# Layer 0's output projection by seven products, two buffers of q and k, and neighbours by row maxima

## The chip, the cores and the metric

The kernel runs on one core of a Trainium2 chip. The time is that of one execution on the device, in microseconds (us). A core has TensorE (PE: matmuls, with PEld for its weight loads), VectorE (DVE), ScalarE (ACT), GpSimd (POOL) and SyncE (SP), which here only issues DMAs. Each engine runs its own instructions in order and waits for others on semaphores.

## The reference

64 graphs of 256 nodes with 512 features go through two attention layers, each with a layer norm and a ReLU ahead of it and a residual behind it. Layer 0 has 4 heads of 64 and sees the adjacency; layer 1 has 8 heads of 64 and sees the adjacency and the node itself. Cut to what matters:

```python
h = maximum(layernorm(x), 0)                     # [64, 256, 512]
q, k, v = h @ Wq, h @ Wk, h @ Wv                 # 4 heads of 64
sim = where(adj, q k^T / 8, -max)                # a node without neighbours attends to all alike
x = x + softmax(sim) v @ Wo + bo
h = maximum(layernorm(x), 0)
h = layernorm(h) * gamma + beta
q, k, v = split(h @ w_qkv.T)                     # 8 heads of 64
scores = where(adj | eye, q k^T / 8, -1e9)
x = x + softmax(scores) v @ w_out.T + b_out
```

All is float32. A row of layer 0 whose node has no neighbour gives equal weights over all 256 nodes.

## The kernel before

Two graphs make a step, so there are 32 steps. All matmuls are float32, except those on the adjacency, which is turned in bfloat16. Scores are kept transposed, keys on the partitions; a mask of 0 or -1e30 is added (`mask_scores`, L795), then come the exponentials (L800), the sum of the two halves of keys (`key_halves`, L808), the products with v (`weigh`, L817), the sums over keys by a matmul with ones (L837), the reciprocals (`invert`, L847, with a check of the greatest sum, L848), their spread over the partitions by eight DMAs on SP (L859) and the scaling of the output (`normalise`, L864). A pair of heads is a unit: two in layer 0, four in layer 1.

A projection of 512 inputs over two graphs is a 2 x 2 block product, and where the kernel says "by seven products" it is done by a scheme of seven block products for eight. `PRODUCT` names the two blocks of each, `weight_sum` and `act_sums0`, `act_sums1` form the sums of blocks that it needs (L404 to L412), `evacuate` and `accumulate` add each product up from its PSUM bank. `SHARED` lets products 2, 4 and 3 accumulate on the banks of 1, 7 and 5, once those have been evacuated. There are four such banks (`m0` to `m3`), which sums, transposes and products take in turn, and four more for scores. Before the change this scheme serves q and k of both layers, v of layer 1 and the combination of layer 1 (`combine1`); v of layer 0 and the combination of layer 0 (`combine0`) are plain matmuls.

The mask of layer 0 needs to know which nodes have neighbours: `masks` sums the turned adjacency over the keys with a matmul by ones (L517), makes the mask `n0` from it on VectorE (L524), and a row `ne` of 0 and 1 (L527) by which q of layer 0 is multiplied on GpSimd (L694).

The order of the work on PE, DVE, ACT and POOL is written out by hand. `at(period, place, fn)` notes a call at a place on a line of time; a step has the length `PERIOD` of places; the list is sorted by place, and the instructions are issued in that order on each engine. A place is thus an order, not a time. `visit(period, w, prev, cur)` weighs one unit and scores the next: six visits lie in a period, and between them lie the sets of seven products (`at_set`). In one period three steps are in work: step s in its layer 1, step s+1 in its combination of layer 0 and its second norms, step s+2 in its norm, projections and first scores of layer 0. `act`, `sm`, `io`, `stat` are pools of SBUF, in which `bufs` is the number of buffers of a name. After the steps, a flag read from the check of sums starts `general_path`, a plain second program, only if a sum had grown beyond a limit.

Of the kernel before, what the change touches and what calls it, by code (L numbers as in the profile page):

```python
# [315 lines left out]
def fast_path(  # L316
# [38 lines left out]
    stat = ctx.enter_context(tc.tile_pool(name="stat", bufs=4))  # L355
    ps_sc = ctx.enter_context(tc.tile_pool(name="ps_sc", bufs=4, space=bass.MemoryType.PSUM))
# [20 lines left out]
    onesb = const.tile([P, P], BF, name="onesb")  # L377
    nc.vector.memset(onesb, 1.0)
# [17 lines left out]
    B_OF = ((0, 8, 7), (1, 3, 1))  # L396
    PRODUCT = {1: (0, 0), 2: (1, 1), 3: (6, 2), 4: (3, 6), 5: (2, 3), 6: (4, 4), 7: (5, 5)}
# [8 lines left out]
    def act_sums0(b, eng=nc.gpsimd):  # L406
        eng.tensor_tensor(b[:, 3], b[:, 7], b[:, 0], ALU.subtract)

    def act_sums1(b, eng=nc.gpsimd):
        eng.tensor_tensor(b[:, 4], b[:, 2], b[:, 3], ALU.subtract)  # L410
        eng.tensor_tensor(b[:, 5], b[:, 2], b[:, 7], ALU.subtract)
        eng.tensor_tensor(b[:, 6], b[:, 1], b[:, 4], ALU.subtract)  # L412
# [3 lines left out]
    HC, HP1 = NC // 2, PR1 // 2  # L416
    wqk0 = const.tile([P, NB, HC, 2, H0], FP, name="wqk0")
    wv0 = const.tile([P, NC, I0], FP, name="wv0")
    wo0 = const.tile([P, PR0, D], FP, name="wo0")
# [6 lines left out]
    def first_weights():  # L426
        for i in range(2):
            for k, w in enumerate((wq, wk)):
                nc.sync.dma_start(
                    wqk0[:, 2 * i:2 * i + 2, :, k, :].rearrange("p j c o -> p (j c) o"),  # L430
                    w[:, i * H0:(i + 1) * H0].rearrange("(c p) o -> p c o", p=P),
                )
        nc.sync.dma_start(wv0, wv.rearrange("(c p) o -> p c o", p=P))
        nc.sync.dma_start(wo0, wo.rearrange("(c p) o -> p c o", p=P))
        for v, t in ((bo, bo_b), (b_out, bout_b)):
            nc.sync.dma_start(t, bass.AP(tensor=v.tensor, offset=v.offset, ap=[[0, P], [1, D]]))
        gbr = sm.tile([2 * NC, P], FP, name="gbr", tag="inv", bufs=1)
        nc.scalar.dma_start(gbr[:NC], gamma.rearrange("(c p) -> c p", p=P))
        nc.scalar.dma_start(gbr[NC:], beta.rearrange("(c p) -> c p", p=P))
        return gbr  # L440
# [57 lines left out]

    def adjacency_turn(s):
        adb = S[s]["adb"]  # L500
        pa = mm_tile([P, NIC, G, N], BF)
        for g in range(G):
            for kc in range(NIC):
                for ic in range(NIC):
                    nc.tensor.transpose(  # L505
                        pa[:, kc, g, ic * P:(ic + 1) * P],
                        adb[:, g * NIC + ic, kc * P:(kc + 1) * P], identb,
                    )
        S[s]["adT"] = act.tile([P, NIC, G, N], BF, name="adT", tag="ab")
        nc.scalar.copy(S[s]["adT"], pa)  # L510

    def masks(s):
        st = S[s]
        adT = st["adT"]
        dg = mm_tile([P, G, N])
        for kc in range(NIC):
            nc.tensor.matmul(dg, onesb, adT[:, kc], start=(kc == 0), stop=(kc == NIC - 1))  # L517
        n1 = st["n1"] = act.tile([P, NIC, G, N], BF, name="n1", bufs=3)
        n0 = st["n0"] = act.tile([P, NIC, G, N], BF, name="n0")
        ne = st["ne"] = act.tile([P, T], FP, name="ne")  # L520
        nc.gpsimd.tensor_scalar(n1, adT, -1.0, BIG, op0=ALU.add, op1=ALU.mult)

        for kc in range(NIC):
            nc.vector.scalar_tensor_tensor(  # L524
                n0[:, kc], dg, 0.5, n1[:, kc], op0=ALU.is_gt, op1=ALU.mult
            )
        nc.vector.tensor_scalar(ne, dg.rearrange("p g n -> p (g n)"), 1.0, None, op0=ALU.min)  # L527
        for kc in range(NIC):
            v = n1[:, kc, :, kc * P:(kc + 1) * P]
            nc.gpsimd.tensor_tensor(v, v, offdiag, ALU.mult)  # L530


    def moments(mv, src, t):
        bs = stat.tile([P, 6], FP, name="bs")
        nc.vector.bn_stats(bs, src[:, t, :])  # L535
        nc.vector.bn_aggr(mv[:, t, 0:2], bs)

    def row_scales(s, var):

        st = S[s]  # L540
        st["r"] = stat.tile([P, NT], FP, name="r", bufs=3)
        st["mr"] = stat.tile([P, NT], FP, name="mr", bufs=3)
        nc.gpsimd.tensor_tensor(st["r"], var, mhalf, ALU.pow)
        nc.gpsimd.tensor_scalar(
            st["mr"], st["mean"][:, :, 0], -1.0, 0.0, op0=ALU.mult, op1=ALU.add
        )
        nc.gpsimd.tensor_tensor(st["mr"], st["mr"], st["r"], ALU.mult)  # L547
# [8 lines left out]
    def norm0(s, t):  # L556
        st = S[s]
        if t == 0:
            st["mean"] = stat.tile([P, NT, 2], FP, name="mv0", bufs=2)
        moments(st["mean"], st["h"], t)  # L560
        if t == NT - 1:
            ve = stat.tile([P, NT], FP, name="ve0", bufs=2)
            nc.gpsimd.tensor_scalar(
                ve, st["mean"][:, :, 1], EPS, 1.0, op0=ALU.add, op1=ALU.mult
            )
            row_scales(s, ve)
# [3 lines left out]
    def norm1(s, t):  # L570
        st, x1 = S[s], S[s]["xt"]
        if t == 0:
            st["mv"] = stat.tile([P, NT, 3], FP, name="mv1", bufs=2)
            st["mean"] = stat.tile([P, NT, 2], FP, name="mg", bufs=2)
            st["h"] = act.tile([P, NT, D], FP, name="h")
# [9 lines left out]
    def norm1_rest(s, t):  # L585
        st = S[s]
        mv, mg, h = st["mv"], st["mean"], st["h"]
        moments(mg, h, t)
        if t == NT - 1:
            ve = stat.tile([P, NT], FP, name="ve1", bufs=2)  # L590
# [81 lines left out]
    def project_qk(s, lyr, a, n):  # L672
# [3 lines left out]
        if n == 1:  # L676
            for pr in (a, a + half):
                st["qk", lyr, pr] = sm.tile([P, 2, T], FP, name="qk", bufs=3)
# [53 lines left out]
    def combine0(s, t):  # L732
        st = S[s]
        bank = mm_tile([P, D])
        for pr in range(PR0):
            nc.tensor.matmul(  # L736
                bank, st["oT0"][:, pr, t // NIC, t % NIC * P:(t % NIC + 1) * P], wo0[:, pr, :],
                start=(pr == 0), stop=(pr == PR0 - 1),
            )
        return lambda: nc.vector.tensor_tensor(st["xt"][:, t, :], bank, st["xt"][:, t, :], ALU.add)  # L740

    def combine1(s, n):
        st = S[s]
        if n == 1:
            st["u"] = sm.tile([P, NIC, HD], FP, name="u", bufs=1)
        bank, first = bank_of(st, "c", n, HD)
        wa, ba = PRODUCT[n]
        for t in range(NIC):
            for c in range(HP1):
                nc.tensor.matmul(  # L750
                    bank[:, t, :], st["oT1"][:, ba, c, t * P:(t + 1) * P], wo1[:, wa, c, :],
                    start=first and (t, c) == (0, 0), stop=(t, c) == (NIC - 1, HP1 - 1),
                    skip_group_check=True,
                )
        return lambda: accumulate(n, bank, token_rows(st["xt"], HD), st["u"], s == NSTEP - 1)
# [54 lines left out]
    def weigh(s, lyr, pr, first):  # L810
# [11 lines left out]
        if lyr == 0:  # L822
            if first:
                st["oT0"] = act.tile([P, PR0, G, N], FP, name="oT0")
            dst = st["oT0"][:, pr]
        else:
            if first:
                st["oT1"] = act.tile([P, NB + 1, HP1, N], FP, name="oT1")
            b0, b1, step = B_OF[pr // HP1]
            dst = st["oT1"][:, b0:b1:step, pr % HP1, :]  # L830
# [39 lines left out]
    PERIOD = 6.13  # L870
# [17 lines left out]
    SETC = (1, 5, 2, 6, 7, 3, 4)  # L888

    def visit(period, w, prev, cur):  # L890
# [7 lines left out]
        if 0 <= cur[0] < NSTEP:  # L898
# [4 lines left out]
            at(period, w + 0.18, exponentials, *cur, 1)  # L903
            at(period, w + 0.2, key_halves, *cur, 0)
            at(period, w + 0.3, key_halves, *cur, 1)

    AT_C0, AT_Q0, AT_V0, AT_H1, AT_C1 = 3.0, 3.57, 4.57, 5.13, 5.131
    for s in range(-1, NSTEP):
# [6 lines left out]
        visit(p, AT_Q0 + 2 / 7, (s, 1, 1, False), (s, 1, 3))  # L915
# [8 lines left out]
    for s in range(NSTEP):  # L924
# [6 lines left out]
        for t in range(NT):  # L931
            at(p, 0.5 + 0.4 * t if s != 1 else 1.8 + 0.2 * t, norm0, s, t)
            at(p, 2.3 + 0.1 * t if s != 1 else 2.6 + 0.1 * t, scale_row, s, t)
        at(p, (3.146, 3.584)[s] if s < 2 else 2.2, adjacency_turn, s)
        at(p, (3.3, 3.727)[s] if s < 2 else 2.75, masks, s)
        for c in range(NC):
            at(p, AT_C0 + 0.14 * (c // 2) + 0.001 * c, transpose_h, s, 0, c)
        at(p, AT_C0 + 0.1, lambda s=s: act_sums0(S[s]["hT"]))
        at(p, AT_C0 + 0.2, lambda s=s: act_sums1(S[s]["hT"]))
# [7 lines left out]
        at(p, 1.8 if s else 0.8, first_bias, s)  # L947
        for t in range(NT):
            at_dense(p, AT_C0 + 0.01 + 0.14 * t, 0.14, combine0, s, t)
            at(p, AT_C0 + 0.3 + 0.14 * t, norm1, s, t)  # L950
            at(p, (3.55, 3.7, 4.05, 4.2)[t], norm1_rest, s, t)
            at(p, 3.62 + 0.08 * t, second_bias, s, t)
            at(p, 4.5 + 0.1 * t, scale_row, s, t)
# [10 lines left out]
        if s < NSTEP - 1:  # L964
            at(p, AT_C1 + 0.1, lambda s=s: act_sums1(S[s]["oT1"]))
            at_set(p, AT_C1, SETC, combine1, s)
            at(p, 6.3, store, s)
        else:
            at(p, AT_C1 + 0.4, lambda s=s: act_sums1(S[s]["oT1"], nc.vector))
            at_set(p, AT_C1, (1, 5, 2, 3, 6, 7, 4), combine1, s)  # L970
# [5 lines left out]
    for i in range(4):  # L976
        at(-2, 2.75, weight_sum, nc.vector, wqk0, i)
    at(-2, 3.5, lambda: blocks.extend(weight_loads()))
# [63 lines left out]
```

## Time and profile before

| | before |
|---|---|
| median of 3 runs | 3436.38 us (3435.82 to 3436.41) |
| profiled execution, its time | 3435.47 us |
| its span, first to last instruction | 3433.7 us |
| granted TensorE clock | 0.997 |
| PE busy | 3391.8 us, 99% of the span |
| VectorE, GpSimd, ACT busy | 1916.3, 1919.4, 1245.3 us |
| records of the combinations: L736, L750 | 512 of 128x512, 1792 of 128x256 |
| records of the neighbours' matmul: L517 | 64 of 128x512 |

A record of PE is half a float32 matmul: L736 has 8 matmuls a step and 16 records. Rows of engines overlap: a "busy" of PE runs on into the next row, so what a piece of work takes is read from the start of one row to the start of the next. "L736 PE MATMUL mm<-wo,oT" reads: line 736, engine, operation, what is written and what is read. In the waits, "A <- B" is time in which A's engine stood still until B was done. In the table of stretches, the pairs after the length are busy time and number of instructions of PE, PEld, DVE, ACT and POOL, followed by the clock, the share of the DMA engines and GB/s.

### The profile page before, as it was taken

The page shows a single profiled execution, that of the slowest core. Times are in us where ns is not written, and L with a number is a line of the kernel's source. Part 1 is how long each engine was busy: PE and PEld are TensorE (multiplying, and loading weights), DVE is VectorE, ACT ScalarE, POOL GpSimd, SP SyncE. Part 2 cuts the span into 40 slices and gives each one's busy share as a digit, 9 for nine tenths or more (in the row PEclk, how much of TensorE's full clock was granted, in tenths as well). Part 3 has the DMA queues.
Part 4 walks back from the last instruction along what each step waited for, and adds up shares of the span by engine and source line. Part 5 has one row for each costly group of instructions (what it writes and reads, how often), then busy time and mean ns, then how long its engine had stood idle before and what let it go on. Part 6 is the DMA issues. An engine that isn't in the chain of part 4 may idle for free.

```text
span 3433.7 us, 59040 instructions
## 1 busy us (share of the span) xinstructions
PE 3391.8 (99%) x22658; PEld 2632.4 (77%) x22658; DVE 1916.3 (56%) x3410; ACT 1245.3 (36%) x2197; POOL 1919.4 (56%) x1790
## 2 busy tenths in 40 slices
PE   8999999999999999999999999999999999999998
PEld 6787777787777877777777778777777777787766
DVE  5655556555565555565555655555655556555544
ACT  3433443333333334433333333344333333333321
POOL 4656565565655566555656555565556565555640
PEclk9999999999999999999999999999999999999999
DMA  3111111111011111111111111111111101111011
GB/s 128 40 53 55 43 40 42 55 55 53 27 45 52 54 55 42 41 42 55 53 54 28 45 52 55 55 37 46 42 54 54 53 29 44 53 54 53 17 41 38
DMA packets 147536, 165.96 MB, mean 48 GB/s; under 512 B 43304, under 2 KB 96048, under 8 KB 147248
## 3 DMA queue, kind: packets, MB, share of 16 engines
q1 hardware_dynamic: 144928, 157.79, 15.4%
q8 instruction: 181, 2.97, 0.4%
q10 hardware_dynamic: 2320, 4.33, 0.4%
q14 instruction: 107, 0.88, 0.1%
HBM read 78.12 MB, written 33.55 MB: 33 GB/s over the span
## 4 chain that ended last, share of the span: by engine, by line
PE 97%; DVE 1%; POOL 1%; ACT 0%; issue 0%; DMA 0%; ACTq 0%; SPq 0%; DVEq 0%; POOLq 0%
PE mm L684 34%; PE mm L725 11%; PE mm L750 11%; PE sc L782 10%; PE sc L817 10%; PE mm L711 6%; PE mm L736 6%; PE mm L603 3%; PE mm L837 2%; PE mm L505 0%; PE mm L517 0%; DVE inv L847 0%; DVE bs L535 0%; SPq L859 0%; ACTq L456 0%
## 5 line engine op out<-in xcount | busy, mean ns | idle before, releaser
L808 POOL TENSOR_TENSOR pd<-p 128x512 f32<-128x512 f32 x380 | 477.7, 1272 | 807.1 <-ACT p L800 706.6
L684 PE MATMUL mm<-hT,wqkv 128*128 128x256 f32 x3584 | 802.0, 381 | 0.0
L684 PEld LDWEIGHTS mm<-hT,wqkv 128*128 128x128 f32 x3584 | 673.9, 190 | 111.0 <-issue 20.9
L800 ACT ACTIVATE p<-p 128x512 f32<-128x512 f32 x768 | 458.9, 629 | 458.8 <-DVE p L795 457.9
L847 DVE RECIPROCAL inv<-mm 128x128 f32<-128x128 f32 x384 | 339.7, 926 | 341.8 <-PE mm L837 324.5
L795 DVE TENSOR_TENSOR p<-sc,n 128x512 f32<-128x512 f32 x768 | 481.2, 682 | 4.5 <-PE sc L782 4.5
L831 ACT COPY oT<-sc 128x512 f32<-128x512 f32 x192 | 112.3, 585 | 1021.1 <-PE sc L817 1021.1
L684 PE MATMUL mm<-hT,wqk 128*128 128x256 f32 x1792 | 401.6, 381 | 3.4 <-ACT qk L618 1.5
L750 PE MATMUL mm<-wo,oT 128*128 128x256 f32 x1792 | 398.0, 383 | 5.0 <-DVE oT L864 3.4
L725 PE MATMUL mm<-wqkv,hT 128*128 128x256 f32 x1792 | 395.3, 381 | 0.0
L684 PEld LDWEIGHTS mm<-hT,wqk 128*128 128x128 f32 x1792 | 337.6, 190 | 72.3 <-DVE inv L847 9.9
L782 PE MATMUL sc<-qk 64*128 64x256 f32 x3072 | 384.9, 390 | 1.9 <-ACT oT L831 1.4
L750 PEld LDWEIGHTS mm<-wo,oT 128*128 128x128 f32 x1792 | 341.4, 192 | 52.6 <-DVE oT L864 4.2
L725 PEld LDWEIGHTS mm<-wqkv,hT 128*128 128x128 f32 x1792 | 338.0, 190 | 55.1 <-issue 10.6
L817 PE MATMUL sc<-p,v 128*32 128x256 f32 x6144 | 374.5, 382 | 5.2 <-ACT p L800 5.2
L782 PEld LDWEIGHTS sc<-qk 64*128 64x128 f32 x3072 | 281.7, 187 | 106.9 <-issue 77.6
L817 PEld LDWEIGHTS sc<-p,v 128*32 128x32 f32 x6144 | 180.4, 109 | 171.0 <-issue 62.2
L864 POOL TENSOR_TENSOR oT<-oT,invb 128x512 f32<-128x512 f32 x190 | 241.8, 1273 | 90.9 <-DMA invb<-inv 86.7
L652 POOL TENSOR_TENSOR xt<-xt,u 128x512 f32<-128x512 f32 x93 | 118.0, 1269 | 245.6 <-DVE xt L645 184.2
L554 ACT ACTIVATE h<-h,mr,r 128x512 f32<-128x512 f32 x252 | 197.4, 808 | 123.9 <-POOL mr L547 123.9
L736 PE MATMUL mm<-wo,oT 128*128 128x512 f32 x512 | 230.4, 593 | 0.0
L711 PE MATMUL mm<-wv,hT 128*128 128x256 f32 x1024 | 230.3, 382 | 0.0
(103 smaller groups left out, 3617.4 us busy)
## 6 DMA issues: line engine op xcount, KB each, us to landing
invb<-inv SPq DMA_DIRECT2D x1532, 32.0 KB, 1.8
xt<-in_x_dram SPq DMA_DIRECT2D x32, 1024.0 KB, 5.4
h<-in_x_dram SPq DMA_DIRECT2D x31, 1024.0 KB, 5.3
out_dram<-xt SPq DMA_DIRECT2D x31, 1024.0 KB, 4.8
ad<-in_adj_dram SPq DMA_DIRECT2D x32, 128.0 KB, 4.4
wr<-in_L_gnn_w_qkv_dram ACTq DMA_DIRECT2D x3, 1024.0 KB, 13.5
h<-in_x_dram SPq DMA_DIRECT2D x4, 256.0 KB, 3.5
wr<-in_L_gnn_w_out_dram ACTq DMA_DIRECT2D x1, 1024.0 KB, 17.3
```

Of the source, the lines that this page charges most:

```text
L684: nc.tensor.matmul(bank[:, k, :], w[:, wa, c, k, a * P:(a + 1) * P], st["hT"][:, ba, c, :], start=first and (k, c) == (0, 0), stop=(k, c) ...
L711: nc.tensor.matmul(bank, st["hT"][:, b0 + t // NIC * step, c % HC, i:i + P], wv0[:, c, :], start=(c == 0), stop=(c == NC - 1),)
L725: nc.tensor.matmul(bank[:, t, :], st["hT"][:, ba, c, t * P:(t + 1) * P], wqkv1[:, wa, c, 2, :], start=first and (t, c) == (0, 0), stop=(t, ...
L736: nc.tensor.matmul(bank, st["oT0"][:, pr, t // NIC, t % NIC * P:(t % NIC + 1) * P], wo0[:, pr, :], start=(pr == 0), stop=(pr == PR0 - 1),)
L750: nc.tensor.matmul(bank[:, t, :], st["oT1"][:, ba, c, t * P:(t + 1) * P], wo1[:, wa, c, :], start=first and (t, c) == (0, 0), stop=(t, c) ...
L782: nc.tensor.matmul(sc[g][e][:, kc, :], qk[rows, 1, k0:k0 + P], qk[rows, 0, g * N:(g + 1) * N], start=True, stop=True,)
L795: nc.vector.tensor_tensor(p[e][:, g], sc[e], neg[:, :, g, :], ALU.add)
L800: nc.scalar.activation(p[e][:, g], p[e][:, g], AF.Exp, scale=SCALE)
L808: engine_of(s, lyr, pr).tensor_tensor(pd[:, e], p[e][:, :, 0, :], p[e][:, :, 1, :], ALU.add)
L817: nc.tensor.matmul(po[r0:r0 + 32, g, :], st[f"v{lyr}"][:, g * NIC + kc, pr * P + r0:pr * P + r0 + 32], p[r0 // DH][:, g, kc, :], start=(kc ...
L847: nc.vector.reciprocal(inv[:, i * P:(i + 1) * P], sums[:, i * P:(i + 1) * P])
L864: engine_of(s, lyr, pr).tensor_tensor(dst, dst, invb, ALU.mult)
```

## The change

The combination of layer 0 is done by seven products too: `combine0` and `combine1` become one `combine`. `wo0` grows to seven blocks of 128x256, of which VectorE makes three at the start, and so does `oT0`, whose sums GpSimd makes before the combination. `oT1` falls from eight blocks to seven. A product of layer 0 is two matmuls of 128x256, and it adds to `xt` through `u`, as in layer 1.

Neighbours are found by a maximum over each row of the adjacency on VectorE (`neighbours`), written to DRAM and read back as one row on all partitions by two DMAs on SP (`spread_neighbours`). The mask `n0` becomes a product on GpSimd.

q and k have two buffers in place of three. The visit that scores the last unit of layer 1 stood two products into the set of q and k of layer 0; it now stands ahead of that set. The places around it move: the four transposes stand together, the combination comes after them, the norms of x1 come behind the visit in the order of rows 2, 3, 0, 1, the second bias goes to the next visit. At the start, `wv0`, `wo0` and the two biases are loaded over ACT's queue.

```diff
-    onesb = const.tile([P, P], BF, name="onesb")
-    nc.vector.memset(onesb, 1.0)
+    O_OF = ((0, 6, 5), (1, 3, 1))
...
-        eng.tensor_tensor(b[:, 3], b[:, 7], b[:, 0], ALU.subtract)
+        eng.tensor_tensor(b[:, 3], b[:, 7 if b.shape[1] > NB else 5], b[:, 0], ALU.subtract)
...
-    wo0 = const.tile([P, PR0, D], FP, name="wo0")
+    wo0 = const.tile([P, NB, HP0, HD], FP, name="wo0")
...
-        nc.sync.dma_start(wv0, wv.rearrange("(c p) o -> p c o", p=P))
-        nc.sync.dma_start(wo0, wo.rearrange("(c p) o -> p c o", p=P))
+        nc.scalar.dma_start(wv0, wv.rearrange("(c p) o -> p c o", p=P))
+        for i in range(2):
+            nc.scalar.dma_start(
+                wo0[:, 2 * i:2 * i + 2].rearrange("p j c o -> p (j c) o"),
+                wo[:, i * HD:(i + 1) * HD].rearrange("(c p) o -> p c o", p=P),
+            )
         for v, t in ((bo, bo_b), (b_out, bout_b)):
-            nc.sync.dma_start(t, ...)
+            nc.scalar.dma_start(t, ...)
...
+    def neighbours(s, g):
+        st = S[s]
+        if g == 0:
+            st["any"] = stat.tile([P, NT], BF, name="any_of", bufs=2)
+        rows = slice(g * NIC, (g + 1) * NIC)
+        nc.vector.tensor_reduce(
+            st["any"][:, rows], st["ad"][:, rows], axis=mybir.AxisListType.X, op=ALU.max
+        )
+
+    def spread_neighbours(s):
+        row = dram.tile([NT, P], BF, name="row")
+        nc.sync.dma_start(row.rearrange("t p -> p t"), S[s]["any"])
+        ne = S[s]["ne"] = act.tile([P, T], BF, name="ne")
+        nc.sync.dma_start(ne, bass.AP(tensor=row.tensor, offset=row.offset, ap=[[0, P], [1, T]]))
...
     def masks(s):
-        dg = mm_tile([P, G, N])
-        for kc in range(NIC):
-            nc.tensor.matmul(dg, onesb, adT[:, kc], start=(kc == 0), stop=(kc == NIC - 1))
...
         for kc in range(NIC):
-            nc.vector.scalar_tensor_tensor(
-                n0[:, kc], dg, 0.5, n1[:, kc], op0=ALU.is_gt, op1=ALU.mult
+            nc.gpsimd.tensor_tensor(
+                n0[:, kc].rearrange("p g n -> p (g n)"),
+                n1[:, kc].rearrange("p g n -> p (g n)"), st["ne"], ALU.mult,
             )
-        nc.vector.tensor_scalar(ne, dg.rearrange("p g n -> p (g n)"), 1.0, None, op0=ALU.min)
...
+    NORM1 = (2, 3, 0, 1)
...
-                st["qk", lyr, pr] = sm.tile([P, 2, T], FP, name="qk", bufs=3)
+                st["qk", lyr, pr] = sm.tile([P, 2, T], FP, name="qk", bufs=2)
...
-    def combine0(s, t):
-        bank = mm_tile([P, D])
-        for pr in range(PR0):
-            nc.tensor.matmul(
-                bank, st["oT0"][:, pr, t // NIC, t % NIC * P:(t % NIC + 1) * P], wo0[:, pr, :],
-                start=(pr == 0), stop=(pr == PR0 - 1),
-            )
-        return lambda: nc.vector.tensor_tensor(st["xt"][:, t, :], bank, st["xt"][:, t, :], ALU.add)
-
-    def combine1(s, n):
+    def combine(s, lyr, n):
+        oT, w, half = st[f"oT{lyr}"], (wo0, wo1)[lyr], (HP0, HP1)[lyr]
         bank, first = bank_of(st, "c", n, HD)
         wa, ba = PRODUCT[n]
         for t in range(NIC):
-            for c in range(HP1):
+            for c in range(half):
                 nc.tensor.matmul(
-                    bank[:, t, :], st["oT1"][:, ba, c, t * P:(t + 1) * P], wo1[:, wa, c, :],
+                    bank[:, t, :], oT[:, ba, c, t * P:(t + 1) * P], w[:, wa, c, :],
...
-    PERIOD = 6.13
+    PERIOD = 6.2
+    SETC0 = (1, 6, 5, 2, 7, 3, 4)
...
-            at(period, w + 0.18, exponentials, *cur, 1)
-            at(period, w + 0.2, key_halves, *cur, 0)
+            at(period, w + 0.22, exponentials, *cur, 1)
+            at(period, w + 0.23, key_halves, *cur, 0)
...
-    AT_C0, AT_Q0, AT_V0, AT_H1, AT_C1 = 3.0, 3.57, 4.57, 5.13, 5.131
+    AT_C0, AT_Q0, AT_V0, AT_H1, AT_C1 = 3.0, 3.64, 4.64, 5.2, 5.201
...
-        visit(p, AT_Q0 + 2 / 7, (s, 1, 1, False), (s, 1, 3))
+        visit(p, AT_Q0, (s, 1, 1, False), (s, 1, 3))
...
+        for g in range(G):
+            at(p, (1.8, 2.7)[s] if s < 2 else 0.58 + 0.14 * g, neighbours, s, g)
+        at(p, (1.81, 2.71)[s] if s < 2 else 0.75, spread_neighbours, s)
...
-            at(p, AT_C0 + 0.14 * (c // 2) + 0.001 * c, transpose_h, s, 0, c)
+            at(p, AT_C0 + 0.001 * c, transpose_h, s, 0, c)
         at(p, AT_C0 + 0.1, lambda s=s: act_sums0(S[s]["hT"]))
-        at(p, AT_C0 + 0.2, lambda s=s: act_sums1(S[s]["hT"]))
+        at(p, AT_C0 + (0.2 if s < 2 else 0.35), lambda s=s: act_sums1(S[s]["hT"]))
...
-            at_dense(p, AT_C0 + 0.01 + 0.14 * t, 0.14, combine0, s, t)
-            at(p, AT_C0 + 0.3 + 0.14 * t, norm1, s, t)
-            at(p, (3.55, 3.7, 4.05, 4.2)[t], norm1_rest, s, t)
-            at(p, 3.62 + 0.08 * t, second_bias, s, t)
-            at(p, 4.5 + 0.1 * t, scale_row, s, t)
+        place = 1.75 if s else 2.48
+        at(p, place, lambda s=s: act_sums0(S[s]["oT0"]))
+        at(p, place + 0.01, lambda s=s: act_sums1(S[s]["oT0"]))
+        for i, n in enumerate(SETC0):
+            at_dense(p, AT_C0 + 0.14 + i / 14, 1 / 14, combine, s, 0, n)
+        for t in range(NT):
+            at(p, (3.79, 3.8, 3.93, 3.94)[t], norm1, s, t)
+            at(p, (4.075, 4.22, 4.23, 4.36)[t], norm1_rest, s, t)
+            at(p, AT_V0 + 0.01 * t, second_bias, s, t)
+            at(p, 4.6 + 0.1 * t, scale_row, s, t)
...
+        at(-2, AT_V0, weight_sum, nc.vector, wo0, i)
```

## The prediction

> **What bounds the kernel now.** I read the page first, then the waits of TensorE, then the busy times of whole steps, then one step in order of time.
>
> ```profile
> PE 3391.8 (99%) x22658; PEld 2632.4 (77%) x22658; DVE 1916.3 (56%) x3410; ACT 1245.3 (36%) x2197; POOL 1919.4 (56%) x1790
> PE 97%; DVE 1%; POOL 1%; ACT 0%; issue 0%; DMA 0%; ACTq 0%; SPq 0%; DVEq 0%; POOLq 0%
> 400.00:505.70 105.70, 105.70 (x713) 82.38 (x712) 59.03 (x105) 39.30 (x69) 61.16 (x58) 1.00 0.16 47
> 1700.00:1805.70 105.70, 105.70 (x710) 82.31 (x709) 59.58 (x107) 38.72 (x68) 60.80 (x58) 1.00 0.16 47
> PE mm L603 <- ACT h L554: 15.9, 7, 10.2
> ```
>
> The chain that ended last is 97% TensorE. In the stretches of one step (columns: length, busy time of PE, PEld, DVE, ACT, POOL, clock, DMA share, GB/s) PE is busy all the time, VectorE and GpSimd 56 to 58%. The waits of PE put 15.9 us on L603, 10.2 of them one wait at the start; between 200 and 3250 us no PE row waits for anything. One step, from L817 at 1199.51 to the same row at 1725.10 five steps on, is 525.59 / 5 = **105.12 us**; 32 of them are 3364, and start and end make up the rest of 3433.7. So work taken from PE is worth its full price, unless another engine then becomes late. The place to look is the timeline of PE around the combination (start, length, counts):
>
> ```profile
> 1725.10 1.93 PE L817 MATMUL sc<-p,v 128*32 128x256 f32 x32
> 1726.86 0.61 PE L837 MATMUL mm<-pd,ones 128*32 128x256 f32 x8
> 1727.40 2.00 PE L782 MATMUL sc<-qk 64*128 64x256 f32 x16
> 1729.33 1.09 PE L603 MATMUL mm<-ident,h 128*128 128x128 f32 x8
> 1730.26 1.88 PE L736 MATMUL mm<-wo,oT 128*128 128x512 f32 x4
> 1731.98 1.04 PE L603 MATMUL mm<-ident,h 128*128 128x128 f32 x8
> 1732.85 5.32 PE L736 MATMUL mm<-wo,oT 128*128 128x512 f32 x12
> 1738.00 3.62 PE L684 MATMUL mm<-hT,wqk 128*128 128x256 f32 x16
> 1741.55 1.93 PE L817 MATMUL sc<-p,v 128*32 128x256 f32 x32
> ...
> 1767.59 12.25 PE L750 MATMUL mm<-wo,oT 128*128 128x256 f32 x56
> 1779.77 1.93 PE L817 MATMUL sc<-p,v 128*32 128x256 f32 x32
> ```
>
> Start to start is what a piece costs: L736 takes 1.72 + 5.15 = 6.87 us, the four transposes 0.93 + 0.87 = 1.80, the layer-1 combination by seven products 12.18.
>
> [...] L808 is 1272 ns in the mean whatever runs beside it. [...] the trace has 1.8 us for `invb`. [...] no 2-byte run is in this trace.
>
> **The change part by part.** Times of a step; "place" is the kernel's own order, one unit some 17 us.
>
> (1) Combination by seven products. PE: 7 products x 2 matmuls of 128x256; in layer 1 four take 12.18/7 = 1.74, so two take 0.87 and the set 6.09: **-0.78**. VectorE: 4 additions of 0.68 go, 6 of 0.69 come, +1.4. ACT: +0.58 (copy into `u`). GpSimd: 3 additions of `u` at 1.27, and 4 block sums of 128x256 before them (no such f32 row; 0.67 by L530, bounds 0.6 and 1.27): +6.5.
>
> (2) Neighbours. PE: L517 goes, 1723.28 - 1722.85 = **-0.43**. VectorE: two L524 (0.69) and L527 (0.68) go; two reductions of 2x256 bytes come, 0.72 each by the slope of the two reductions in the trace (353 at 192, 279 at 128; bounds 0.35 and 1.4). They sit where VectorE idled 1.94 and 1.10 us before evacuations, so nobody waits. GpSimd: two products of 128x512 bf16, 1.27 each (bounds 0.67 and 1.34), in front of the `offdiag` rows, which ended 5.6 us before GpSimd's next work. SP: two DMAs at 0.75, the second waiting for the first. Behind them on SP are the eight `invb` DMAs of visit 1.0 (590 ns each to issue), whose `inv` is ready some 6 us after the first can go. A landing of 1.7 us (fastest `invb`) to 5.4 us (a 1 MB load) fits: cost 0, cover 6 us.
>
> (3) Four transposes in one run instead of two and two: 1.75 (layer 1 at 1765.84 to 1767.59) for 1.80: **-0.05**. But their four evacuations on ACT now precede the first exponentials.
>
> (4) The visit. With two buffers of q and k the scores of unit (1,3) must precede product 1 of the next set; the visit goes ahead of products 1 and 6. Nothing is added: the weighing, the sums, the scores, `invert`, four mask additions, four exponentials and eight DMAs move up 3.5 us on PE, VectorE, ACT and SP, and on GpSimd two key halves and a `normalise`. PE then writes new q and k only after these scores, so the lost buffer costs nothing.
>
> (5) The norms of x1 move behind that visit, rows 2,3,0,1; the second bias (4 x 1.24) moves to the next visit on GpSimd. There it pushes key halves from 8.1 to 12.2 us after the weighing, and block sums of oT1 to 17.2; the product that needs the last of them starts at 22. Free.
>
> (6) Exponentials of graph 1 from +0.18 to +0.22. In visit 2 the `adT` copy (1.01) now precedes them, and the key halves end some 2 us later; GpSimd has that slack until the next `normalise` chain.
>
> Sum of the saving: 0.78 + 0.43 + 0.05 = **1.26 us a step, 40.3 in 32 steps**.
>
> **What comes back.** The stretch of 16.6 us behind the combination is the tight one already (same columns):
>
> ```profile
> 1725.10:1738.00 12.90, 12.90 (x89) 7.47 (x89) 9.78 (x19) 5.75 (x11) 5.51 (x6) 1.00 0.09 22
> 1738.00:1754.60 16.60, 16.60 (x113) 13.03 (x111) 12.45 (x25) 6.76 (x13) 12.94 (x16) 1.00 0.07 18
> ```
>
> I laid the new queues out with the durations of the rows, 0 at the weighing of visit 3.0.
> ACT: `oT` copy 2.0; four relus 4.9 to 7.0; exponentials to 8.05; `u` copy 8.03 to 8.60; exponentials to 9.7. Product 2 reuses the bank of product 1 at 5.98 + 3 x 0.87 = 8.59: PE waits 0.07. Product 7's evacuation must end before product 4, one product (0.87) on: 0.15 (lag in L750's rows) + 0.69 + 0.06 = 0.90, so 0.03 more.
> GpSimd: key halves 9.2 to 11.65, three sums of hT to 15.3, `normalise` to 16.6, `u` additions to 17.85, 19.1, 20.35.
> PE: combination ends at 12.2; weighing, scores, and then the set of q, k for 12.3.
> VectorE from 14.7: `invert` 2.15, four masks 2.40, so the first norm at 19.28, its rows complete at 19.1: a margin of 0.2. Then two norms 1.62, one evacuation 0.60, two norms, one evacuation, three second moments 2.43, evacuation of product 7 at 26.3 to 27.0; PE wants that bank at 27.07. **Margin about zero.**
> The last second moments end at 27.75; then the chain of tiny GpSimd rows and `ne`:
>
> ```profile
> 1752.48 0.19 POOL L591 TENSOR_SCALAR ve<-mv 128x4 f32<-128x4 f32 x1
> ...
> 1753.03 1.02 POOL L543 TENSOR_TENSOR r<-ve,mhalf 128x4 f32<-128x4 f32 x1
> ...
> 1754.55 1.28 POOL L694 TENSOR_TENSOR qk<-qk,ne 128x512 f32<-128x512 f32 x1
> ```
>
> It takes 2.07 + 1.28 and ends at 31.1; the scores that read it start at 31.1, where before they had 1.07 us (1755.83 to 1756.90). Again no margin.
> So 0.1 a step is sure and each tie may cost up to 0.3; I take 0.2 for them together. (0.1 + 0.2) x 30 = 9 back.
>
> **Start.** `wv0`, `wo0` and the biases (1.5 MB) move from SP behind `wqk0` to ACT's queue at once, beside `h`. [...] The trace has 1 MB of `h` landed some 5 us after 0.74; up to 1 MB beside it could delay it by 3. I take +2.5, bounds -1 and 6. SP is held there by the row of neighbours; `h` of step 1 is wanted at 14.1 only.
>
> Sum against the profiled execution: 3435.5 - 40.3 + 9 + 2.5 = 3406.7. It stands 0.9 under the median, so **3408**.
>
> **Rivals.** (A, 0.58) The above: 3396 (nothing back) to 3415. (B, 0.20) The ties give way by 0.6 to 1.0 a step, because VectorE, continuously busy from 14.7 to 30, is the bound of that stretch: 3436.4 - 40.3 + 2.5 + 30 x 0.7 to 1.0 = 3420 to 3429. Against it: PE's waits of a stretch also give VectorE time. (C, 0.14, slower) GpSimd's additions of `u` come behind key halves, three sums and `normalise`, VectorE stops at the first norm for them, behind it stand the evacuations of products 6 and 5, and PE runs out of banks. It decides from 1.2 us a step; if each of the nine GpSimd rows ahead came 0.27 later, or the exponentials 2.4 us later, less the 0.2 of margin, PE would lose about 2.2: 3436.4 + 2.5 + 30 x 2.2 - 40.3 = 3465. For it: margins of 0.2 and 0; against it: rows of 1257 to 1293 ns, no more, in the whole trace. (D, 0.08) B and a bad start cancel the gain: 3430 to 3443. That the new neighbours are not found, so that the second program follows, I give under 0.01.
>
> **Numbers.** About 0.2% (7 us) is what a measurement of this kernel can tell from no change. Faster is A and B, 0.78; same 0.08; slower 0.14. The range, 3397 to 3436, takes A, B and the nearer half of D; A alone is 3396 to 3415.
>
> **What would show it.** Right: L736 and L517 gone; L750 or its successor with 2688 records; a step of 104.0 to 104.4 us; PE with small waits for ACT `u`, the evacuation of product 7, or GpSimd's `qk`, 0.1 to 0.4 us a step. B or C: VectorE rows of the first norm idle before GpSimd's `xt`, PE's L684 waiting for VectorE. Wrong altogether: a step over 105.1 us, or PE waiting for the mask through the row DMA, which I cost at nothing.

## The result, and the profile after

| | before | after |
|---|---|---|
| median | 3436.1 us (3433.78 to 3436.41, 4 runs) | 3526.88 us (3522.1 to 3537.2, 4 runs) |
| profiled execution, its span | 3435.47, 3433.7 us | 3524.76, 3523.0 us |
| PE busy, granted clock | 3391.8 us, 0.997 | 3395.4 us, 0.987 |

The change is **slower**: 1.027 of the time before, 95% interval 1.0246 to 1.0294, or 91 us. The forecast was 3408, a gain of 28 us.

The page of the changed kernel, busy times and the chain that ended last by engine and by line:

```profile
PE 3395.4 (96%) x22978; PEld 2714.9 (77%) x22978; DVE 1933.3 (55%) x3445; ACT 1232.2 (35%) x2229; POOL 2183.6 (62%) x2078
...
PE 72%; DMA 16%; SPq 4%; DVE 3%; issue 2%; POOL 2%; ACT 1%; DVEq 0%; ACTq 0%; POOLq 0%
PE mm L704 26%; PE mm L761 16%; DMA row<-any_of 12%; PE sc L829 7%; PE sc L794 7%; PE mm L731 6%; SPq L870 4%; PE mm L745 3%; PE mm L623 3%; PE mm L848 2%; DVE inv L858 2%; DMA invb<-inv 1%; DMA out_dram<-xt 1%; DMA h<-in_x_dram 0%; POOL pd L820 0%
```

TensorE was 97% of the chain and is 72%. A transfer of 1 KB, the row of neighbours on its way to DRAM, is 12% of it. Before the change TensorE had no wait between 200 and 3250 us, and GpSimd waited little for `invb` there (us in total, times, longest):

```profile
POOL oT L864 <- DMA invb<-inv: 57.6, 67, 2.8
```

The waits of the changed kernel in that window, from TensorE's view of them back to the transfer:

```profile
PE mm L704 <- DVE extremes L859: 60.2, 24, 5.2
...
DVE inv L858 <- DMA invb<-inv: 161.4, 22, 10.4
...
POOL oT L875 <- DMA invb<-inv: 407.3, 36, 17.5
...
SPq L518 <- DMA row<-any_of: 500.5, 28, 21.3
```

Read upwards: SP stands 17.9 us in the mean (500.5 / 28) at its second DMA, `ne<-row`, until the first has landed. The `invb` DMAs are queued behind it. GpSimd's `normalise` waits for them, and so do VectorE's reciprocals, because `inv` has one buffer. On VectorE stand behind the reciprocals the check L859, which reads the bank of sums, the masks and the evacuations; TensorE wants that bank for product 5 of q and k of layer 1. One such place, in the timelines of SP, GpSimd, VectorE and TensorE of the changed kernel (start, length, in brackets the idle time before and its releaser):

```profile
1861.15 0.37 SPq L516 DMA_DIRECT2D row<-any_of  x1
1861.61 0.46 SPq L485 DMA_DIRECT2D ad<-in_adj_dram  x1
1882.28 0.34 SPq L518 DMA_DIRECT2D ne<-row  x1
...
1889.69 1.26 POOL L875 TENSOR_TENSOR oT<-oT,invb 128x512 f32<-128x512 f32 x1 [16.34 <-DMA invb<-inv]
...
1889.70 1.77 DVE L858 RECIPROCAL inv<-mm 128x128 f32<-128x128 f32 x2 [9.21 <-DMA invb<-inv]
...
1887.47 0.61 PE L526 MATMUL mm<-identb,adb 128*128 128x128 bf16 x8
1892.14 10.56 PE L704 MATMUL mm<-hT,wqkv 128*128 128x256 f32 x40 [4.06 <-DVE extremes L859]
```

The `row` DMA is issued at 1861.15, and SP goes on at 1882.28. The cost is more than the wait. The same piece of work, from the scores to the next weighing, without and with it, and the part of the disturbed one that follows the wait, in two pieces (stretches: length, busy time of PE, PEld, DVE, ACT, POOL, clock, DMA share, GB/s):

```profile
1777.57:1792.63 15.06, 14.98 (x85) 12.37 (x81) 7.34 (x12) 7.30 (x12) 11.40 (x14) 1.00 0.12 29
1881.98:1902.63 20.65, 16.59 (x85) 13.63 (x81) 7.34 (x12) 7.31 (x12) 12.54 (x15) 0.92 0.14 33
...
1892.14:1897.00 4.86, 4.86 (x15) 3.95 (x16) 3.55 (x6) 4.43 (x8) 4.63 (x9) 0.65 0.19 47
1897.00:1902.60 5.60, 5.60 (x27) 4.68 (x25) 1.38 (x2) 2.53 (x4) 5.60 (x5) 1.00 0.02 6
```

It takes 5.6 us longer: 4.2 until product 5 starts, and 1.4 because the clock is low behind the wait. The mean of 0.65 over 4.86 us hides two values: from 1892.50 to 1895.80 the granted clock is 0.50, and the record of that stretch is 3.41 us long. All nine waits of 3.3 to 5.2 us in the window came with such a stretch. Of the shorter ones, waits of 1.95 and 2.55 us, which ended at 270.01 and 1466.09, had a clock of 0.50 behind them too (271.20 to 274.40, 1466.10 to 1469.10), and so had one of 2.32, while those of 2.01, 2.23, 2.49 and 2.96 us had not. So in this trace the length of a wait alone does not tell whether the clock falls.

Between 200 and 3250 us the changed kernel has twelve such stretches, 51 us in all; half of that, up to 26 us, is my estimate of what the clock costs. The kernel with a quick row (e2, below) has none. TensorE is busy 2985.1 of these 3050 us, and all 3050.0 in that other kernel, so 65 us are idle. Together that is some 90 of the 98 us by which the changed kernel is slower than that one once the start is over. (Here and below the start ends with the first sums over keys, some 100 us in, that follow the last transposes of weights.)

Where no stall fell, the combination came out close to the forecast. The transposes start at 1796.85, the combination at 1798.65, the next weighing at 1805.00:

```profile
1796.85 1.97 PE L623 MATMUL mm<-ident,h 128*128 128x128 f32 x16
1798.65 6.42 PE L761 MATMUL mm<-wo,oT 128*128 128x256 f32 x28
1805.00 1.93 PE L829 MATMUL sc<-p,v 128*32 128x256 f32 x32
```

The set takes 6.35 us where the plain one took 6.87; 6.09 and 0.1 for its banks were forecast.

The undisturbed piece, 1777.57 to 1792.63, shows how much TensorE could bear. Ahead of it SP issued `row` at 1756.99 and went on at 1773.45, VectorE's reciprocals waited 4.83 us for `invb`, and TensorE waited for nothing. In four such steps SP stood 15.1 to 15.4 us without any wait of TensorE for the check; the 20.2 us behind 1861.15 cost the 4.06.

### The profile page after: what moved, and what is told of

Its sections match the earlier page's. It is cut to its first block, busy times and chain, and to the rows that moved or that the text cites. A ratio compares the mean times of both kernels' runs of the same rounds, so it can differ in the third digit from the quotient of the medians.

```text
span 3523.0 us, 60226 instructions
## 1 busy us (share of the span) xinstructions
PE 3395.4 (96%) x22978; PEld 2714.9 (77%) x22978; DVE 1933.3 (55%) x3445; ACT 1232.2 (35%) x2229; POOL 2183.6 (62%) x2078
## 4 chain that ended last, share of the span: by engine, by line
PE 72%; DMA 16%; SPq 4%; DVE 3%; issue 2%; POOL 2%; ACT 1%; DVEq 0%; ACTq 0%; POOLq 0%
PE mm L704 26%; PE mm L761 16%; DMA row<-any_of 12%; PE sc L829 7%; PE sc L794 7%; PE mm L731 6%; SPq L870 4%; PE mm L745 3%; PE mm L623 3%; PE mm L848 2%; DVE inv L858 2%; DMA invb<-inv 1%; DMA out_dram<-xt 1%; DMA h<-in_x_dram 0%; POOL pd L820 0%
## 5 line engine op out<-in xcount | busy, mean ns | idle before, releaser
L704 PE MATMUL mm<-hT,wqkv 128*128 128x256 f32 x3584 | 823.7, 390 | 62.9 <-DVE extremes L859 60.2
L704 PEld LDWEIGHTS mm<-hT,wqkv 128*128 128x128 f32 x3584 | 688.9, 195 | 185.5 <-issue 82.5
L761 PE MATMUL mm<-wo,oT 128*128 128x256 f32 x2688 | 601.4, 382 | 4.9 <-DVE oT L875 3.2
L761 PEld LDWEIGHTS mm<-wo,oT 128*128 128x128 f32 x2688 | 502.7, 191 | 85.1 <-DVE xt L661 11.1
L672 POOL TENSOR_TENSOR xt<-xt,u 128x512 f32<-128x512 f32 x189 | 239.0, 1272 | 229.9 <-DVE xt L665 184.5
L661 DVE TENSOR_TENSOR xt<-mm,xt 128x512 f32<-128x512 f32 x128 | 88.2, 689 | 338.9 <-PE mm L761 338.8
```

The costliest lines, as they stand in the source:

```text
L672: (nc.vector if last else nc.gpsimd).tensor_tensor(r, r, u, ALU.add)
L704: nc.tensor.matmul(bank[:, k, :], w[:, wa, c, k, a * P:(a + 1) * P], st["hT"][:, ba, c, :], start=first and (k, c) == (0, 0), stop=(k, c) ...
L761: nc.tensor.matmul(bank[:, t, :], oT[:, ba, c, t * P:(t + 1) * P], w[:, wa, c, :], start=first and (t, c) == (0, 0), stop=(t, c) == (NIC - ...
```

## The experiments

My theory after the result: the two-byte row lands late, and this alone is the loss; the rest of the change saves what was forecast. Rivals: the weights on ACT's queue, the new order of the visit, the reductions, or any row sent through DRAM at that place.

### The row alone in the kernel before (e4)

```diff
+        if s >= 2:
+            for g in range(G):
+                at(p, 0.58 + 0.14 * g, neighbours, s, g)
+            at(p, 0.75, spread_neighbours, s)
```

> The kernel before with the row maxima and the two DMAs on SP added from the third step on, their result not used (and only half of the row read back, for room). Theory 1: SP is held for some 16 us a step here too, PE waits 3 to 5 us in most steps, and the time is 3500 to 3580. Theory 2: nobody waits for it, 3436 to 3445.

Measured: 3525.09 us against 3433.64, ratio 1.0258 (1.0241 to 1.0275), so **+91.5 us** for reductions and two DMAs whose result nobody reads. SP and TensorE of this kernel, waits between 200 and 3250 us:

```profile
SPq L515 <- DMA row<-any_of: 490.1, 28, 19.6
...
PE mm L702 <- DVE extremes L866: 48.1, 26, 3.3
```

The same chain, in the old order, without the weights on ACT's queue and without the seven products in layer 0. Reductions and row together are enough; e2 and e9 below keep the reductions and do not have the loss.

### What in the row costs: four forms of it (e5)

The kernel before again, with the row written in a form that changes from step to step, each waited for on SP by a DMA of one element.

```diff
+        if kind == 0:      # near = [4, 128]: 512 pieces of 2 bytes, side by side
+            nc.sync.dma_start(near.rearrange("t p -> p t"), st["any"])
+        elif kind == 1:    # far = [4, 128, 256]: 512 pieces of 2 bytes, 512 bytes apart
+            nc.sync.dma_start(far[:, :, 0].rearrange("t p -> p t"), st["any"])
+        elif kind == 2:    # whole = [128, 4]: 128 pieces of 8 bytes
+            nc.sync.dma_start(whole, st["any"])
+        else:              # half = [2, 128]: 256 pieces of 2 bytes, side by side
+            nc.sync.dma_start(half.rearrange("t p -> p t"), st["any"][:, :2])
```

> The kernel before with the row maxima and a row written by SP from the third step on, its result not used; step by step the row goes out in one of four forms: 512 pieces of 2 bytes side by side in DRAM; 512 pieces of 2 bytes, 512 bytes apart; 128 pieces of 8 bytes; 256 pieces of 2 bytes. SP then reads one element of it back, which shows how long the landing takes. If the landing goes with the number of pieces: 16, 16, some 4 to 5 and 8 to 9 us. If it is that neighbours of 2 bytes fall into the same stretch of DRAM and queue up behind each other: 16, under 5, some 4 and 8 to 9. If it is a fixed price of any write so small: 16 in all four.

SP's waits in this kernel (us in total, times, longest):

```profile
SPq L530 <- DMA half<-any_of: 152.6, 8, 21.6
...
SPq L518 <- DMA near<-any_of: 133.1, 7, 20.0
...
SPq L526 <- DMA whole<-any_of: 38.6, 8, 6.6
...
SPq L522 <- DMA far<-any_of: 29.3, 7, 5.1
```

One run of it took 3509.23 us. The means are 19.1, 19.0, 4.8 and 4.2 us. It is **not the number of pieces**: 512 of them 512 bytes apart land in 4.2, and 256 side by side take as long as 512. I had expected 8 to 9 for the half row, so that part was wrong. What the two slow forms share is runs of 128 two-byte values next to each other.

Nor is it the moving. The trace has a record of every packet. In all four forms the first packet of the row starts 3.6 to 3.8 us after the issue, behind the 1 MB of `xt` that SP issued some 0.5 us earlier, and the last has ended 4.6 to 4.7 us after it. From there until SP is let on pass, in the mean, 15.3 us for the 512 side by side, 15.5 for the 256, 1.7 for the pieces of 8 bytes and 0.6 for those 512 bytes apart. The changed kernel's DMA engines from 1755 to 1776 us show the same, one digit for 0.525 us, tenths busy:

```profile
DMA  7000913799999402002000200100100000000000
```

The row is issued at 1756.99. The nines are `xt` and `ad`. The last packet of 2 bytes ends at 1762.74, after that the engines do nearly nothing, and SP is let on 10.7 us later. Over the 28 rows between 200 and 3250 us it is the same: the last packet ended 4.9 us after the issue in the mean, and 14.0 us more passed (10.7 to 17.6) before SP went on. The time passes after the last packet, and no record shows what fills it.

### The row turned on TensorE (e2)

```diff
+        turned = mm_tile([NT, P], BF)
+        nc.tensor.transpose(turned, S[s]["any"], identb)
+        ne = S[s]["ne"] = act.tile([P, T], BF, name="ne")
+        nc.scalar.copy(ne[:NT, :P], turned)
         row = dram.tile([NT, P], BF, name="row")
-        nc.sync.dma_start(row.rearrange("t p -> p t"), S[s]["any"])
-        ne = S[s]["ne"] = act.tile([P, T], BF, name="ne")
+        nc.sync.dma_start(row, ne[:NT, :P])
```

> The changed kernel with the four columns of row maxima turned on PE (one transpose of 128x4 in bfloat16, a copy on ACT) and written to DRAM as 4 rows of 256 bytes, both DMAs still on SP. Theory 1: the row lands in 2 to 3 us, SP is held no longer than that, and the time is 3398 to 3415, with a start earlier than that of the changed kernel by 10 us or more. If the count of pieces isn't what makes the landing long, it stays near 16 us and the time near 3525. Theory 2: 3490 or more.

Beyond the lines shown, the row goes out at place 0.9 for 0.75, behind `ad`.

Measured: 3413.48 us (3412.77 to 3414.17), ratio **0.994** (0.9923 to 0.9957). Four pieces of 256 bytes land so soon that SP waits 2.4 us in the mean; part of the difference to the forms above is that `xt` goes out some 3 us ahead of the row here, not 0.5. Its waits between 200 and 3250 us, and the chain by engine:

```profile
SPq L521 <- DMA row<-ne: 69.3, 29, 3.2
...
PE 97%; DVE 1%; POOL 1%; DMA 0%; ACT 0%; issue 0%; ACTq 0%; SPq 0%; DVEq 0%; POOLq 0%
```

TensorE waits for nothing in that window, and a step is 1804.86 - 1700.78 = 104.08 us for 105.12. Everything else of the change is still there, so none of the other rivals makes the loss.

### The row in pieces of 8 bytes (e9)

The smallest edit: nothing is added, the row only lies otherwise in DRAM, and GpSimd reads every fourth value.

```diff
-        row = dram.tile([NT, P], BF, name="row")
-        nc.sync.dma_start(row.rearrange("t p -> p t"), S[s]["any"])
+        row = dram.tile([P, NT], BF, name="row")
+        nc.sync.dma_start(row, S[s]["any"])
...
+        S[s]["ne"] = ne.rearrange("p (q t) -> p t q", t=NT)
```

> The changed kernel with one thing altered: the row of neighbours lies in DRAM with the four values of a partition side by side, so it is written in 128 pieces of 8 bytes (4.8 us in the mean with the forms compared side by side), and GpSimd reads its columns in that order, every fourth value. No work is added to TensorE. Theory (the landing of the 2-byte neighbours is the whole loss; my step fails only in the landing that it assumed): 4.8 us lies inside the cover of 6 us that the prediction gave, so TensorE shows no waits behind the spread reciprocals between 200 and 3250 us, and the time is 3408 to 3420. Rival (any row written out and read back in this place holds SP too long): waits behind the spread reciprocals stay, 3450 or more. A second way to miss: GpSimd reads every fourth bf16 value slower than 1.16 us for 128x512; if it takes 1.3 to 2.3 us, q comes later to the scores by that much more, and 1 us a step is lost: some 3440.

Measured: **3412.13 us** (3412.06 to 3414.43) against 3434.83, ratio 0.9938 (0.9921 to 0.9954). SP waits 5.5 us in the mean in the same window, and no engine passes it on to TensorE:

```profile
SPq L518 <- DMA row<-any_of: 160.8, 29, 7.4
```

The landing is longer than that of the turned row and the step is the same, 1804.79 - 1700.71 = 104.08 us. So a wait of 5.5 us in the mean, 7.4 at most, is covered. The 6 us that I had read off were the cover of the `invb` DMAs alone: GpSimd and VectorE have slack behind them, and in the changed kernel TensorE began to wait only where SP stood for more than some 15.5 us. GpSimd's q product takes 1.30 us for 1.16, which nobody waits for.

### Both DMAs on ACT's queue (e1)

```diff
-        nc.sync.dma_start(row.rearrange("t p -> p t"), S[s]["any"])
+        nc.scalar.dma_start(row.rearrange("t p -> p t"), S[s]["any"])
...
-        nc.sync.dma_start(ne, ...)      # right behind it
+        nc.scalar.dma_start(ne, ...)    # at place 1.95 in place of 0.75
```

> The changed kernel with both DMAs of the neighbours on ACT's queue, the one that reads the row back issued at place 1.95 in place of 0.75 (3.25 and 3.7 for the first two steps); the row is still written in 512 pieces of 2 bytes. Theory 1 (SP stands behind the landing of the row, some 16 us a step, so that the eight DMAs of invb, then VectorE at the reciprocals, then PE come late): SP has no wait for the row any more, the waits of PE for VectorE L859 go, and the time falls to 3410 to 3428 (a start some 18 us late is left). Theory 2 (the stretch behind the combination, GpSimd and VectorE, is the cause): 3490 or more. Theory 3 (512 tiny writes hold up the other DMAs on the shared engines): invb lands late all the same, 3480 or more.

The first of the two goes out at 0.9 for 0.75.

Missed: 3451.68 us (3448.18 to 3457.2), ratio 1.0047 (1.003 to 1.0064), which is 75 us less than the changed kernel and 38 more than with the turned row. Between 200 and 3250 us TensorE's waits for the check fall from 60.2 to 6.7 us. SP issues neither of the two DMAs and yet waits for the row ahead of `invb` DMAs, over the whole run:

```profile
SPq L873 <- DMA row<-any_of: 127.5, 19, 12.5
```

The semaphores in the trace tell why. In this program the DMAs of SP and ACT take eight landing semaphores in turn (in the kernel before, 210 or 211 of 1684 DMAs each), and SP issues a DMA only when the one that last had its semaphore has landed. At 1713.84 ACT issues the row; the eighth DMA after it is one of SP's for `invb`, and SP stands 10.36 us until 1734.19. In all 19 waits the semaphore is the row's. So it is the program that still ties the two queues, and the row still lands late.

Of the 38 us, 15 lie in the start (it ends at 123.3 for 108.3), with TensorE waiting for relus and copies of ACT.

### The matmul of neighbours back (e3)

Layer 0 by seven products and the new order stay; `masks` is that of before with L517, and the reductions and the row go.

```diff
+        dg = mm_tile([P, G, N])
+        for kc in range(NIC):
+            nc.tensor.matmul(dg, onesb, adT[:, kc], start=(kc == 0), stop=(kc == NIC - 1))
...
-        at(p, (1.81, 2.71)[s] if s < 2 else 0.75, spread_neighbours, s)
```

> The changed kernel with its way of finding neighbours undone: the matmul by ones, the mask n0 and the row ne on VectorE as before, no row DMA (ne is kept in bfloat16, and offdiag is one block used twice, for room). Theory 1: the combination by seven products and the moved visit do what was forecast, 0.83 us a step less 0.3 given back, so 3413 to 3427, a few us of it from the loads at the start. Theory 2: the stretch behind the combination is the cause, so it stays at 3490 or more.

Measured: 3423.84 us (3422.82 to 3425.88), ratio 0.9969 (0.9956 to 0.9981). From the end of the start to the end of the run it is 3424.1 - 108.33 = 3315.8 us, where before has 3433.7 - 99.60 = 3334.1: 18.3 less. My terms for what it keeps are 40.3 - 9 - 0.43 x 32 = 17.5. This is the part of the change that pays without the row.

### Product 7 ahead of product 2 (e7)

In the two kernels with a quick row a small wait is left: TensorE's weight loads stop at product 2, whose bank ACT still copies into `u`, and at a later product whose bank VectorE still adds to `xt`. The kernel with the turned row, 200 to 3250 us:

```profile
PEld mm L764 <- DVE xt L664: 9.3, 29, 0.3
PEld mm L764 <- ACT u L660: 4.5, 29, 0.2
```

```diff
-    SETC0 = (1, 6, 5, 2, 7, 3, 4)
+    SETC0 = (1, 6, 5, 7, 2, 3, 4)
```

> The kernel with the row turned on PE (e2_turned_row), with the products of layer 0's combination in the order 1, 6, 5, 7, 2, 3, 4 in place of 1, 6, 5, 2, 7, 3, 4, so that a product lies between the end of 7's and the start of 4's use of their bank, and two between 5 and 3 and between 6 and 2. If the waits of the weight loads at these banks (0.3 us a step for VectorE, 0.15 for ACT's copy of u) are what made the set 6.35 us long instead of 6.09: the set falls to 6.1 and the time by 5 to 12 us, to 3402 to 3409. If not: 3411 to 3415.

Measured, on top of the turned row: **3405.92 us** (3405.53 to 3406.46) against 3433.92, ratio 0.9918 (0.9901 to 0.9934). Both waits are gone. The timeline of TensorE:

```profile
1719.80 6.21 PE L764 MATMUL mm<-wo,oT 128*128 128x256 f32 x28
1725.93 1.93 PE L832 MATMUL sc<-p,v 128*32 128x256 f32 x32
```

The set takes 6.13 us for 6.35; 0.22 x 30 is 6.6 of the 7.6 us between the two kernels. This version beats both, the kernel before and the changed one.

### The start (e6, e8, e10, e11)

With a quick row the start still ends at 108.3 us, where before has 99.6. Four kernels tried to win that back: weights and biases on SP again (e6 on the turned row, e8 with the order of e7 too), and beside it the maxima of step 0 behind its transposes (e10; e11 with the row in 8-byte pieces).

```diff
-        nc.scalar.dma_start(wv0, ...)        # also wo0, bo, b_out
+        nc.sync.dma_start(wv0, ...)
...
-            at(p, (1.8, 2.7)[s] if s < 2 else 0.58 + 0.14 * g, neighbours, s, g)
-        at(p, (1.81, 2.71)[s] if s < 2 else 0.9, spread_neighbours, s)
+            at(p, (2.95, 2.7)[s] if s < 2 else 0.58 + 0.14 * g, neighbours, s, g)
+        at(p, (3.21, 2.71)[s] if s < 2 else 0.9, spread_neighbours, s)
```

> The kernel with the row turned on PE (e2_turned_row), with wv0, wo0 and the two biases loaded on SP behind wqk0 again. If the loads side by side on two queues are what made its start 8.7 us later than before: the first sums of the unit after the start come 5 to 9 us earlier, and the time falls from 3413.5 to 3404 to 3409. If something else in the start is the cause (the second DMA of the row on SP, the mask by GpSimd): 3411 to 3415.

> e2_turned_row with both: the loads on SP and the order 1, 6, 5, 7, 2, 3, 4. If the two are independent and both as expected: 3394 to 3404.

> The kernel with the turned row, product 7 ahead of product 2 and the weights and biases on SP, with the start altered: the maxima of step 0 come after its transposes, and its row goes out behind the load of h of step 1. Theory (the start is late because the row of step 0 stands ahead of the first transposes on VectorE, ACT and PE, and ahead of h of step 1 on SP): the first transposes begin at 10.3 as in the kernel before, h of step 1 is issued at about 14.1, the first product does not wait for VectorE behind the norm, and the first sums of the visit behind the weights come at 100 to 102 instead of 108: 3397 to 3401. Rival (h of step 1 lands late beside the 4 MB of weights whenever it is issued): 3405 to 3407.

> The changed kernel with the row in 8-byte pieces, product 7 ahead of product 2, the weights and biases on SP, and the altered start. If both theories hold, it has the start of the kernel before and no transpose of the row on TensorE (one 128x4 bf16 transpose a step, some 0.1 us with its place in the queue): 3392 to 3400. If GpSimd is slow on every fourth value, it stands above the kernel with the turned row and the altered start.

All four missed: 3414.03 (3413.37 to 3415.6), 3406.83 (3406.16 to 3407.07), 3409.46 (3407.99 to 3410.02) and 3408.64 us (3406.16 to 3409.1). In e6 and e10 the first transposes begin at 10.27 and 10.38 us as before, 4.5 us sooner than in e2, and the gain is given back at once. TensorE of e10 at the start:

```profile
10.38 3.96 PE L626 MATMUL mm<-ident,h 128*128 128x128 f32 x16 [10.38 <-ACT h L574]
...
29.79 3.75 PE L707 MATMUL mm<-hT,wqk 128*128 128x256 f32 x8 [3.79 <-DVE qk L647]
36.61 3.79 PE L797 MATMUL sc<-qk 64*128 64x256 f32 x16 [3.07 <-POOL qk L717]
```

VectorE stands with that evacuation behind the norm of step 1, whose `h` is late; SP of e10 shows why:

```profile
15.24 0.38 SPq L485 DMA_DIRECT2D ad<-in_adj_dram  x1
15.73 0.44 SPq L483 DMA_DIRECT2D h<-in_x_dram  x1
16.47 0.33 SPq L520 DMA_DIRECT2D row<-ne  x1
25.73 0.36 SPq L521 DMA_DIRECT2D ne<-row  x1
```

The adjacency of step 1 goes ahead of `h` on SP. In the kernel before it went at 10.26 and `h` at 14.14; now it waits until VectorE's maxima have read the one buffer of step 0's, and `h` follows at 15.73 and lands at 27.4, beside 4 MB of weights issued from 15.48 on. The row of step 0, put behind `h`, then takes 9 us itself, and the product that makes q comes late for the scores (3.07 us). The start of e10 ends at 111.10, not at the 100 to 102 expected.

That is not the whole of the start, though. The kernel with the matmul of neighbours back (e3) has neither maxima nor row, and its start ends at 108.33 all the same. In all kernels here that have the new order and the seven products, TensorE waits some 4 us for ACT's `h` at the transposes just ahead of the end of the start. Before, and in e3:

```profile
94.37 0.59 PE L603 MATMUL mm<-ident,h 128*128 128x128 f32 x2 [0.71 <-ACT h L554]
96.12 1.80 PE L603 MATMUL mm<-ident,h 128*128 128x128 f32 x14 [1.16 <-ACT h L554]
...
100.50 0.33 PE L629 MATMUL mm<-ident,h 128*128 128x128 f32 x1 [4.07 <-ACT h L577]
...
105.53 2.98 PE L835 MATMUL sc<-p,v 128*32 128x256 f32 x32
```

From the scores ahead of these transposes to the end of the start it takes 8.6 us before (90.98 to 99.60) and 13.9 in e3 (94.43 to 108.33): 5.3 of the 8.7 us lie here. The norms of x1 come later in the new order, which would make this `h` late; no run changed it, so that is argued. Of the rest, the weights' queue alone moved nothing (108.22 in e6 for 108.31). Which order would win the start back wasn't found.

## Why the prediction was wrong, point by point

**The failed step is (2), its DMAs on SP: "cost 0, cover 6 us".** The working was right up to the landing. The wait, the eight `invb` DMAs behind it and their cover were named, and e9 shows that 5.5 us of waiting cost nothing. The landing was taken from `invb` and a 1 MB load, 1.7 to 5.4 us; SP stood 17.9 us in the mean. The cover was mis-sized too, to the safe side: TensorE bore some 15.5 us. I had said that the trace has no 2-byte run, and then bounded it by rows with pieces of 1 KB and more. A range from nearest rows is no bound where they differ from the case in the size of the pieces and in how these lie. Nor was it small pieces as such: three forms, of 2, 8 and 256 bytes, landed in 2.4 to 5.5 us. What counted in e5 is how the pieces lie, 19 us for 2 bytes side by side and 4.2 apart. An `invb` took 1.8 us from issue to landing; of the row's time in the changed kernel 14.0 us in the mean passed after its last packet. The changed kernel less the turned row is 3526.9 - 3413.5 = **113 us**, and 13.9 of it (122.17 - 108.31) lies in the start. My list of what would show the forecast wrong had "PE waiting for the mask through the row DMA"; TensorE waited through the `invb` DMAs queued behind it.

**The saving held.** The forecast was -40.3 + 9 = -31.3 us outside the start. The turned row has 3411.0 - 108.31 = 3302.7 from the end of the start on, for 3334.1: **-31.4**. A step is 104.08, inside the 104.0 to 104.4 given. That the sums agree to 0.1 us is luck: a step saved 1.04 us where 1.26 - 0.3 = 0.96 was forecast, and this kernel has a transpose of the row that the forecast did not have.

**The ties held, in other places.** I had 0.07 and 0.03 us a step for the banks of products 2 and 4 and 0.2 for the rest. The weight loads waited 4.5 / 29 = 0.16 and 9.3 / 29 = 0.32 at the two banks; the tie of q with the scores cost 11.9 / 29 = 0.4 of weight loads and no wait of TensorE. The set was 0.26 us longer than 6.09, and e7 won 0.22 of it back. Rival B's 0.6 to 1.0 did not come (its sum began at 0.7; from 0.6 it would begin at 3417).

**Rival C did not occur.** Between 200 and 3250 us TensorE waits for nothing of GpSimd's, and for VectorE's evacuations 3.1 us in all, where the rival needed 2.2 us a step. The slower side came by another road: the same engine and the same blocked evacuations, but through the reciprocals.

**The start was undersized**: +2.5, bounds -1 to 6. It is +8.7 with a quick row and +22.6 with the slow one. I counted the weights beside `h`, by an estimate, but their return to SP moved nothing (e6), and I had no term for the last transposes ahead of its end, where 5.3 us of it lie. I wrote that SP "is held there by the row" but `h` "is wanted at 14.1 only", and missed that the adjacency of step 1, which SP issues ahead of `h`, waits for the maxima.

**Small terms**: a maximum over 2 x 256 bytes took 0.67 us (forecast 0.72), a product of 128x512 bf16 on GpSimd 1.16 (1.27), block sums of 128x256 in float32 0.74 (0.67).

## What to carry to other kernels

Before a tiny transfer is put ahead of others on a queue, ask how its pieces lie at the other end, not only how many bytes it has: the same 1 KB took 19.0 us or 4.2 in e5. Here it was enough to let a partition's values stay together (SP waited 5.5 us for 17.9), or to turn them on the chip first (2.4). If no row of the trace has that layout, price it as unknown up to the cover and beyond, and let that case have its own chance. A wait inside a queue costs what stands behind it, so follow it through every single-buffered tile to the engine that bounds the kernel.

## What the runs showed of the hardware

- A row written from SBUF to DRAM in one place of the kernel (e5), until the next DMA may read it: 256 or 512 two-byte values side by side 19 us, 512 of them 512 bytes apart 4.2, 128 pieces of 8 bytes 4.8. The last packet ended 4.6 to 4.7 us after the issue in all four; from there until SP was let on passed 15.3 to 15.5 us for values side by side, 0.6 for those 512 bytes apart and 1.7 for the pieces of 8 bytes.
- A wait of TensorE of 4.06 us cost 5.6: the clock after it was 0.50 for 3.4 us. Waits of 1.95, 2.32 and 2.55 us had 0.50 behind them too; four of 2.01 to 2.96 us had not.
- A float32 product on GpSimd of 128x512 took 1.30 us for 1.16 where one of its inputs was read at every fourth bfloat16 value (e9); an all-bfloat16 one with the same input took 1.16 both ways.
